# Later layernorms and transposes, token splits one per product, weight sums behind residual sums: an adaLN transformer block on one core

## The chip, the core and the metric

The kernel runs on one core of a Trainium2 chip. The metric is the device time of one execution in microseconds; several executions are timed and the median is taken. Beside them one execution is recorded by the hardware profiler; all views of the profile below are of that one.

The engines go by their short names: PE is TensorE (matmuls and transposes), DVE is VectorE, ACT is ScalarE, POOL is GpSimd, and SP is the engine whose queue issues nearly all transfers (DMAs). Each engine has a queue of its own and takes its instructions in that order. An instruction that waits holds up all that stands behind it on the same engine.

## What is computed

A transformer block with adaptive layernorm, for 2 batches of 1024 tokens of 1024 features, all in float32. Cut to what matters here:

```python
mod = (_silu(c) @ wmod).reshape(2, 6, 1, -1)
sa, ca, ga, sb, cb, gb = (mod[:, i] for i in range(6))      # ga, gb: kept at least 0.25 in size
h = _layernorm(x) * (1 + ca) + sa
x = x + ga * attention(h)
h = _layernorm(x) * (1 + cb) + sb
x = x + gb * ffn(h)

def attention(h):                       # 32 heads of 32, ALiBi bias, causal
    q, k, v = split(clip(h @ Wqkv.T, -8, 8))
    q, k = layer_norm(q) * q_ln_w + q_ln_b, layer_norm(k) * k_ln_w + k_ln_b
    return softmax(q @ k.T * scale + slopes * rel, causal) @ v @ Wout.T

def ffn(h):                             # 2752 inner features; Wg, Wu, Wd hold -1, 0, 1
    return ((silu(h @ Wg.T * ag) * (h @ Wu.T * au)) @ Wd.T) * ad
```

## The kernel before

**Products in seven.** Each large matrix product is done by a Strassen-Winograd scheme: the operands are cut in 2 by 2 blocks, sums and differences of the blocks are formed on DVE and POOL, and seven block products take the place of eight. `SEVEN` lists them in the order in which they are issued: P1, P2, U2, P5, U3, P53, U6, each with its bank of PSUM (`x` or `y`), its left operand (A11, A12, S2, S1, S3, S4, A22) and its right one (B11, B21, T2, T1, T3, B22, T4). Products of one bank build on each other, so after P1, U2 and P5 a copy on ACT (L972, L1305, L1751) saves the bank before the next product of that bank may start. The other four complete a quarter of the output each, read by DVE (L979, L977, L1313, L1311, L1756).

**Stages.** Modulation vectors; the q, k, v projections of batch 0; then attention of both batches, and beside it on the same engines the "dense" work: the projections of batch 1 and the output product with residual, layernorm and transposes of batch 0 and the first half of batch 1. `together` deals the two out to each other by estimated times. After attention comes the second half of the output product of batch 1 alone, then gate and up for batch 0 and batch 1 (11 "pairs" of 256 inner features each, the last of 192), then the down product.

**Order.** The scheduler of the framework orders the instructions of each engine by the order in which the program emits them and by when it reckons that their inputs are there. Where `pinned[0]` is set, PE keeps the emitted order; that is so from the start of attention on, except in pair 0 of batch 0. `behind(a, b)` adds an edge for that scheduler: `a` comes after `b` on its engine. It puts no wait into the program.

**Layernorm and transposes.** `normalize` takes the statistics of a block of 2 x 128 tokens on DVE (L706, L707) and returns `rest_`: on ACT a logarithm (L713) and an exponential (L717), on DVE five steps on two elements per partition (L711, L719 to L722) and two applies (L724). `Todo` holds what follows: `first` keeps `rest_` back as `due` or runs it at once, `place` runs it, and `run` issues one of the four groups of transposes (four 128 x 128 transposes by `turned`, L743, evacuated by DVE L860 and, in part, by ACT L862). `seven` calls `between` after half a product and after a whole one. `between` places the `due` layernorm at once, and issues transposes from product number `q0` on: 1 for batch 1 and the output product, 3 for the half of the output product after attention. Beside attention there is one PSUM bank for transposes.

**Output product.** `output` handles a block `j` of 256 tokens (four per batch, b and j in the names). `operand` loads the attention output of the next block at product 2 and, at product 6, scales it by the reciprocal sums (L1248) and forms its sums on DVE and POOL (L1249 to L1253). `read` multiplies by the gate and adds to the residual on POOL (L1314, L1315). The sum is stored, normalized, and transposed; `token_operands` forms the token side of gate and up from it (T1, T2 on DVE, T3, T4 on POOL, L1199 to L1202) and stores all seven operands on SP's queue (L1205).

**Attention.** `scores` issues the score products, exponentials (L1080) and, on diagonal blocks, a causal mask on POOL (L1084; the last one is kept in `last_mask`). `weigh` multiplies by v and adds the probabilities up on DVE and POOL (L1112).

**Gate and up.** Before each pair `weight_operands` turns the loaded weights into seven operands: three casts on ACT (L1635, L1636, L1643) and four sums on POOL (L1637, L1640 to L1642). For the very first pair the sum S1 goes behind `last_sum`, the last sum of the operand formed last. `tokens_in` loads one token operand (1 MB) on SP, casts it on ACT (L1549, the high part) and subtracts on DVE (L1550, the low part); both parts are multiplied. Batch 0's seven come from `token_tiles` while the output product of the last block runs, as its buffers come free. Batch 1's seven are emitted at the start of `gate_up(1)`, into the same buffers. Of the products of a pair, P2, P53, U3 and U6 give the four activation blocks; they and their sums (L1715) are stored on SP. `last_read` and `last_copy` remember the last bank read on DVE and the last bank copy on ACT, and `hold` puts an instruction behind `last_read`; only the checks of the weights use them.

The lines that set the places:

```python
def between(q):
    side(order.index(q))
    self.place()
    if order.index(q) >= q0:
        yield from self.run(n)
```

## Time and profile before

| | us |
|---|---|
| median of 3 runs | 2305.59 |
| their range | 2300.73 to 2306.57 |
| the profiled execution's own time | 2305.24 |
| its span, first to last instruction | 2303.5 |
| PE busy | 2159.4 (94%) |
| DVE busy | 1340.7 (58%) |
| POOL busy | 1106.8 (48%) |
| ACT busy | 944.7 (41%) |
| mean granted TensorE clock | 0.978 |

In the profile, stages can be told by the names of tiles: `bank<-wB,a` and `bank<-wT,a` are projections, `sc` and `av` scores and values, `bank<-wT_o,ao..` the output product, `gx`, `gy`, `ux`, `uy` gate and up, `dx`, `dy` the down product. Attention runs from about 360 to 1346 us, the output product of batch 1's last two blocks from 1351 to 1435, gate and up from 1416 to 2017, the down product from there to the end. A line of the timeline gives start, duration, engine, source line, operation, tiles, how many instructions were merged, and in brackets the idle time of the engine before it and what ended that.

### The profile page before, as it was taken

To read this page: it belongs to the slowest core of one execution; us is meant where nothing else is said; L and a number is where in the kernel's file an instruction comes from. 1 tells how busy PE (TensorE), PEld (TensorE's weight loads), DVE (VectorE), ACT (ScalarE), POOL (GpSimd) and SP (SyncE) were. 2 spreads that over 40 slices of the span, in tenths; PEclk is the share of its full clock that TensorE was granted. 3 is DMA by queue.
4 is the path that set the end of the run, shared out by engine and by line. 5 is a ranking of instruction groups with operands and counts; after the bars stand their busy time and mean duration, and the time that the engine had idled before them with its cause. 6 is when DMAs were issued, how large, how long until landed. Compare 5 with 4: busy or idle time off the path is not lost.

```text
span 2303.5 us, 27279 instructions
## 1 busy us (share of the span) xinstructions
PE 2159.4 (94%) x9537; PEld 1180.6 (51%) x9537; DVE 1340.7 (58%) x1843; ACT 944.7 (41%) x1782; POOL 1106.8 (48%) x775
## 2 busy tenths in 40 slices
PE   6999999999998899998888878899998999999998
PEld 2444443333333333332222234688876888788887
DVE  5775652455645543456557566887877654544544
ACT  1322224445344445555545522655554444323331
POOL 2330202443343464675575646488967767422212
PEclk9999999999999999999999989999999999999999
DMA  9887776536235531864443265778766786598765
GB/s 370 315 290 274 286 286 233 182 132 238 88 110 178 166 119 48 281 172 135 117 129 110 75 165 176 253 220 267 226 219 208 252 272 214 179 388 314 271 233 185
DMA packets 319350, 482.45 MB, mean 209 GB/s; under 512 B 16092, under 2 KB 235036, under 8 KB 310244
## 3 DMA queue, kind: packets, MB, share of 16 engines
q1 hardware_dynamic: 316752, 472.19, 60.8%
q10 hardware_dynamic: 2452, 8.43, 1.0%
q8 instruction: 77, 1.26, 0.2%
q14 instruction: 69, 0.57, 0.1%
HBM read 323.01 MB, written 157.55 MB: 209 GB/s over the span
## 4 chain that ended last, share of the span: by engine, by line
PE 40%; POOL 6%; issue 3%; DVE 3%; ACT 2%; DMA 1%; SPq 0%; POOLq 0%; ACTq 0%; DVEq 0%
PE dx L740 7%; PE gx L740 6%; PE ux L740 6%; PE dy L740 5%; PE uy L740 5%; PE gy L740 5%; PE bank L740 3%; PE sc L740 2%; ACT p L1080 2%; POOL p L1112 1%; DVE p L1112 1%; POOL xr L1315 1%; PE av L740 1%; DMA wst<-in_L_ffn_Wu_dram 1%; POOL aS L1715 1%
## 5 line engine op out<-in xcount | busy, mean ns | idle before, releaser
L1080 ACT ACTIVATE p<-sc,kw 128x128 f32<-128x128 f32 (+3 forms) x1024 | 422.5, 515 | 423.0 <-PE sc L740 409.5
L740 PE MATMUL bank<-wT,a 128*128 128x512 f32 x768 | 365.7, 609 | 14.4 <-ACT P L972 7.6
L1112 POOL TENSOR_TENSOR p<-p,p 128x1024 f32<-128x1024 f32 (+3 forms) x128 | 263.6, 2059 | 220.1 <-PE av L740 194.5
L1112 DVE TENSOR_TENSOR p<-p,p 128x1024 f32<-128x1024 f32 (+3 forms) x192 | 242.3, 1275 | 121.4 <-POOL p L1084 65.1
L740 PE MATMUL bank<-wB,a 128*128 128x512 f32 x576 | 275.4, 615 | 1.0 <-DVE raw L977 0.6
L740 PEld LDWEIGHTS bank<-wT,a 128*128 128x128 f32 x768 | 136.5, 191 | 193.9 <-issue 160.7
L1084 POOL TENSOR_SCALAR_AFFINE_SELECT p<-p 128x256 f32<-128x256 f32 x256 | 136.0, 544 | 199.2 <-ACT p L1080 193.1
L740 PE MATMUL sc<-cq,ck 32*128 32x512 f32 (+3 forms) x1536 | 189.3, 536 | 27.4 <-ACT p L1080 27.3
L740 PE MATMUL av<-p,cv 128*32 128x512 f32 (+3 forms) x1536 | 169.6, 505 | 12.1 <-POOL p L1084 12.0
L740 PEld LDWEIGHTS bank<-wB,a 128*128 128x128 f32 x576 | 103.8, 192 | 147.7 <-issue 132.3
L1840 DVE TENSOR_TENSOR lo<-lo,hi 128x1408 fp32r<-128x1408 f32 x56 | 95.0, 1699 | 92.2 <-ACT hi L1839 92.1
L740 PEld LDWEIGHTS sc<-cq,ck 32*128 32x128 f32 x1536 | 64.3, 184 | 164.4 <-issue 92.4
L1839 ACT CAST hi<-lo 128x1408 fp32r<-128x1408 f32 x56 | 76.9, 1375 | 136.9 <-DMA lo<-act 96.7
L1904 POOL TENSOR_TENSOR early_P<-early_P,x1in 128x512 f32<-128x512 f32 x16 | 37.2, 2323 | 164.1 <-DVE early_P L1902 159.4
L1637 POOL TENSOR_TENSOR wS<-wst,wst 128x1024 fp32r<-128x1024 f32 (+1 forms) x22 | 66.9, 3041 | 93.1 <-PE uy L740 72.7
L979 DVE TENSOR_TENSOR raw<-P,bank 128x512 f32<-128x512 f32 x48 | 32.9, 685 | 127.2 <-PE bank L740 117.0
L740 PEld LDWEIGHTS av<-p,cv 128*32 128x32 f32 x1536 | 32.6, 109 | 137.8 <-issue 81.5
L740 PE MATMUL gy<-hs,wS 128*128 128x512 f32 (+1 forms) x352 | 89.5, 396 | 7.9 <-ACT gP L1751 2.7
L740 PE MATMUL ux<-hs,wA 128*128 128x512 f32 (+1 forms) x352 | 88.7, 394 | 3.9 <-DVE uP L1756 3.9
L740 PE MATMUL gx<-hs,wA 128*128 128x512 f32 (+1 forms) x352 | 89.4, 394 | 1.5 <-DVE hs L1550 1.2
L740 PE MATMUL uy<-hs,wS 128*128 128x512 f32 (+1 forms) x352 | 89.3, 397 | 1.2 <-DVE uP L1756 1.2
L740 PE MATMUL gx<-hs,wS 128*128 128x512 f32 (+1 forms) x352 | 87.7, 390 | 2.3 <-ACT gU L1751 1.4
(269 smaller groups left out, 3994.9 us busy)
## 6 DMA issues: line engine op xcount, KB each, us to landing
lo<-act SPq DMA_DIRECT2D x56, 704.0 KB
a<-hop SPq DMA_DIRECT2D x20, 1792.0 KB
wm<-in_L_wmod_dram SPq DMA_DIRECT2D x48, 512.0 KB
act<-aS SPq DMA_DIRECT2D x88, 256.0 KB
wB<-in_L_attn_Wqkv_dram SPq DMA_DIRECT2D x21, 1024.0 KB
wst<-in_L_ffn_Wg_dram SPq DMA_DIRECT2D x40, 512.0 KB
wst<-in_L_ffn_Wu_dram SPq DMA_DIRECT2D x40, 512.0 KB
qk<-qs SPq DMA_DIRECT2D x16, 1024.0 KB
```

The lines of the kernel that those rows point to most:

```text
L740: return in_order(nc.tensor.matmul(*args, **kw_))
L979: nc.vector.tensor_add(dst, part_t[MATE[q]], bank)
L1080: last_exp[0] = nc.scalar.activation(p[:, g, lo:hi], sp[:, g, lo:hi], AF.Exp, bias=kw[:, d, h_ : h_ + 1])
L1084: last_mask[0] = nc.gpsimd.affine_select(out=p[:, :, 0:P], in_=p[:, :, 0:P], pattern=[[0, 2], [1, P]], compare_op=ALU.is_ge, fill=0.0, bas ...
L1112: adders[b](half, jb).tensor_add(dst, dst, ps[half][:, :, 0:n])
L1315: nc.gpsimd.tensor_add(xs[m][:, ts(n, HALF)], xs[m][:, ts(n, HALF)], yg)
L1637: ins = nc.gpsimd.tensor_add(f["S1"], raw["A21"], raw["A22"])
L1715: getattr(eng, op)(act[q], act[x_], act[y_])
L1839: nc.scalar.copy(hi, lo.bitcast(FP))
L1840: nc.vector.tensor_sub(lo, lo.bitcast(FP), hi.bitcast(FP))
L1904: eng.tensor_add(y, y, x1_of.pop(s))
```

## The change

- `normalize`: the small steps are folded. The first one also multiplies by -0.5, and after the exponential three steps follow (two multiplies and a fused add and multiply) where four stood.
- `between` no longer places the layernorm during product 0. `q0` becomes 2 for all projections (but the first of all) and the default of `output`, so transposes there start one product later. `normalize` in `output` runs at once only for batch 1's last block, not for its blocks 1 and 2 too.
- `masked` puts POOL's token sums (T3, T4), operand multiplies and operand sums behind the last mask emitted, while attention runs.
- `tokens_in` only loads; `tokens_split` does the cast and the subtraction, behind the last bank copy and the last bank read. Batch 0: two splits at once, the other five one per product in pair 0, each two products ahead of its use. Batch 1: a load after each product of batch 0's last pair, five splits in that pair and two in the first pair of batch 1.
- `last_sum`, behind which the first weight sum goes, becomes the last residual sum of batch 1's block 2.

```diff
@@ -692,6 +692,12 @@
 
     last_exp = [None]
     last_mask = [None]
+    beside = [False]
+
+    def masked(ins):
+        if beside[0]:
+            behind(ins, last_mask[0])
+        return ins
 
     def normalize(tiles, outs, small, nm):
 
@@ -708,18 +714,16 @@
 
         def rest_():
             ve = small.tile([P, n], FP, tag="ve", name=f"ve_{nm}")
-            nc.vector.tensor_scalar_add(ve, mv[:, :, 1], EPS)
+            nc.vector.tensor_scalar(ve, mv[:, :, 1], EPS, -0.5, ALU.add, ALU.mult)
             lv = small.tile([P, n], FP, tag="lv", name=f"lv_{nm}")
             ln = nc.scalar.activation(lv, mv[:, :, 1], AF.Ln, bias=eps_t)
             if last_exp[0] is not None:
                 behind(ln, last_exp[0])
             rstd = small.tile([P, n], FP, tag="rstd", name=f"rstd_{nm}")
             nc.scalar.activation(rstd, lv, AF.Exp, scale=-0.5)
-            fix = small.tile([P, n], FP, tag="fix", name=f"fix_{nm}")
-            nc.vector.tensor_mul(fix, rstd, rstd)
-            nc.vector.tensor_mul(fix, fix, ve)
-            nc.vector.tensor_scalar(fix, fix, -0.5, 1.5, ALU.mult, ALU.add)
-            nc.vector.tensor_mul(rstd, rstd, fix)
+            nc.vector.tensor_mul(ve, ve, rstd)
+            nc.vector.tensor_mul(ve, ve, rstd)
+            nc.vector.scalar_tensor_tensor(rstd, ve, 1.5, rstd, ALU.add, ALU.mult)
             for m, (t, o) in enumerate(zip(tiles, outs)):
                 nc.vector.tensor_scalar(o, t, mv[:, m, 0:1], rstd[:, m : m + 1], ALU.subtract, ALU.mult)
 
@@ -904,7 +908,8 @@
 
             def between(q):
                 side(order.index(q))
-                self.place()
+                if order.index(q) > 0:
+                    self.place()
                 if order.index(q) >= q0:
                     yield from self.run(n)
 
@@ -964,7 +969,7 @@
                     rawp.tile([P, D], FP, tag="raw", name=f"raw_{b}_{part}_{j}_{m}") for m in range(2)
                 ]
                 part_t = {}
-                q0, n = (2 - b, places) if b or part or j else (5, 4)
+                q0, n = (2, places) if b or part or j else (5, 4)
 
                 def read(q, bank):
                     if q in ("P1", "U2", "P5"):
@@ -1198,8 +1203,8 @@
         t = {q: pool.tile([P, KC // 2, P], FP, tag=f"t{q}", name=f"t{q}_{b}_{j}") for q in ("T4", "T3", "T2", "T1")}
         nc.vector.tensor_sub(t["T1"], b12, b11)
         nc.vector.tensor_sub(t["T2"], b22, t["T1"])
-        nc.gpsimd.tensor_sub(t["T3"], b22, b12)
-        nc.gpsimd.tensor_sub(t["T4"], b21, t["T2"])
+        masked(nc.gpsimd.tensor_sub(t["T3"], b22, b12))
+        masked(nc.gpsimd.tensor_sub(t["T4"], b21, t["T2"]))
         t.update(B11=b11, B21=b21, B22=b22)
         for i, q in enumerate(TOKEN_OPS):
             nc.sync.dma_start(hop2_dram[b][:, i, :, j], t[q])
@@ -1217,6 +1222,13 @@
             nc.sync.dma_start(wt_dram[3][:, r, i], w[:, at])
 
     last_sum = [None]
+    last_read = [None]
+    last_copy = [None]
+
+    def hold(ins, last=last_read):
+        if last[0] is not None:
+            behind(ins, last[0])
+        return ins
 
     def operand(b, j, ap_):
 
@@ -1245,12 +1257,14 @@
             nc.sync.dma_start(a[q], ao_dram[b][qb][:, ds(kh * 4, 4), ds(y0 + m * P, P)])
         yield
         for m, kh, q, eng in blocks:
-            eng.tensor_mul(a[q], a[q], rb[:, ds(kh * 4, 4), ts(m, P)])
+            ins = eng.tensor_mul(a[q], a[q], rb[:, ds(kh * 4, 4), ts(m, P)])
+            if eng is nc.gpsimd:
+                masked(ins)
         nc.vector.tensor_add(a["S1"], a["A21"], a["A22"])
         nc.vector.tensor_sub(a["S2"], a["S1"], a["A11"])
         a["S3"] = a["A21"]
-        nc.gpsimd.tensor_sub(a["S3"], a["A11"], a["A21"])
-        last_sum[0] = nc.gpsimd.tensor_sub(a["S4"], a["A12"], a["S2"])
+        masked(nc.gpsimd.tensor_sub(a["S3"], a["A11"], a["A21"]))
+        masked(nc.gpsimd.tensor_sub(a["S4"], a["A12"], a["S2"]))
         made[b, j] = a
         yield
 
@@ -1264,7 +1278,7 @@
 
     later = []
 
-    def output(b, js, pools, banks, bt, todo, keep, q0=1, after=None):
+    def output(b, js, pools, banks, bt, todo, keep, q0=2, after=None):
 
         gap_, ap_, tkp, partp, hbp, sm = pools
         while (b, 2 * js[0] * P // QB) not in settled:
@@ -1312,7 +1326,9 @@
                 else:
                     nc.vector.tensor_add(yg, yg, bank)
                     nc.gpsimd.tensor_mul(yg, yg, ga[:, ts(n, HALF)])
-                nc.gpsimd.tensor_add(xs[m][:, ts(n, HALF)], xs[m][:, ts(n, HALF)], yg)
+                ins = nc.gpsimd.tensor_add(xs[m][:, ts(n, HALF)], xs[m][:, ts(n, HALF)], yg)
+                if (b, j) == (B - 1, NJ - 2):
+                    last_sum[0] = ins
 
             yield from seven(lambda q, i: a[q][:, i, :], bt, banks, read, todo.places(q0, 1, ahead), 2)
             yield from todo.run(len(todo.list), True)
@@ -1321,7 +1337,7 @@
             for m in range(2):
                 nc.sync.dma_start(x1_dram[b * NT + qts[m]], xs[m])
             xn = xs
-            todo.first(normalize(xs, xn, sm, f"f{b}_{j}"), b == 1 and j >= NJ // 2 - 1)
+            todo.first(normalize(xs, xn, sm, f"f{b}_{j}"), b == 1 and j == NJ - 1)
             h2 = keep(b, j)
             for m in range(2):
                 for g in range(2):
@@ -1504,7 +1520,9 @@
             return LEAD + DENSE0 * a / att_us[0]
         return LEAD + DENSE0 + DENSE1 * (a - att_us[0]) / att_us[1]
 
+    beside[0] = True
     together(attention(apools, (halves, mostly), banks), dense_work(), share)
+    beside[0] = False
     att.close()
     opools, _, bt, todo, _ = out_args
     in_range()
@@ -1546,8 +1564,12 @@
         t = hs_tiles[b, i]
         raw = t[:, 1].bitcast(FP)
         token_load[0] = eng.dma_start(raw, hop2_dram[b][:, i].rearrange("p k j t -> p k (j t)"))
-        nc.scalar.copy(t[:, 0], raw)
-        nc.vector.tensor_sub(t[:, 1], raw, t[:, 0].bitcast(FP))
+
+    def tokens_split(b, i):
+        t = hs_tiles[b, i]
+        raw = t[:, 1].bitcast(FP)
+        hold(nc.scalar.copy(t[:, 0], raw), last_copy)
+        hold(nc.vector.tensor_sub(t[:, 1], raw, t[:, 0].bitcast(FP)))
 
     def own(stack, nm, bufs=1):
         return stack.enter_context(tc.tile_pool(name=nm, bufs=bufs, side="right", reuse_waits="tile"))
@@ -1561,6 +1583,8 @@
                 )
         for i in sorted(which):
             tokens_in(0, i)
+        for i in range(2):
+            tokens_split(0, i)
 
     def first_tokens():
         ost.close()
@@ -1576,14 +1600,6 @@
     low.close()
     late_pools.close()
 
-    last_read = [None]
-    last_copy = [None]
-
-    def hold(ins):
-        if last_read[0] is not None:
-            behind(ins, last_read[0])
-        return ins
-
     def small_integers(w, at, pool):
 
 
@@ -1593,9 +1609,7 @@
         j = small[0:n, 0 : int(np.prod(shape))]
         if len(shape) > 1:
             j = j.rearrange("p (a b) -> p a b", a=shape[0])
-        cast = nc.scalar.copy(j, w)
-        if last_copy[0] is not None:
-            behind(cast, last_copy[0])
+        hold(nc.scalar.copy(j, w), last_copy)
         hold(nc.vector.scalar_tensor_tensor(
             j, j, 0.0, w, ALU.add, ALU.not_equal, accum_out=count_a[0:n, at : at + 1]
         ))
@@ -1683,9 +1697,6 @@
 
             def gate_up(b):
                 tiles = [hs_tiles[b, i] for i in range(7)]
-                if b:
-                    for i in range(7):
-                        tokens_in(b, i)
                 for p in range(NPR):
                     n = PAIRS[p][1]
                     if p == 1:
@@ -1717,6 +1728,9 @@
                             keep_act(q, act[q])
 
                     for e, (c_, qa, qb_, q) in enumerate(SEVEN):
+                        split = {(0, 0): (0, e + 2), (0, NPR - 1): (1, e - 2), (1, 0): (1, e + 5)}.get((b, p))
+                        if split is not None and 0 <= split[1] < 7:
+                            tokens_split(*split)
                         if e == 3 and wdst is not None:
                             down_parts(p_, wdst)
                         if e == 4 and nb < B:
@@ -1755,6 +1769,8 @@
                                 t = part[mat, MATE[q]]
                                 last_read[0] = nc.vector.tensor_add(t[0:n], t[0:n], ps[0:n])
                                 done[mat] = t
+                        if (b, p) == (0, NPR - 1):
+                            tokens_in(1, e)
                         if q in QUAD:
                             m, h = QUAD[q]
                             ib = 2 * p + m
```

## The prediction

> **What bounds the kernel now.** I read five views in this order: the summary, the waits by engine, the timeline at each large wait, the windows around them, and the chain of waits.
>
> ```profile
> PE 40%; POOL 6%; issue 3%; DVE 3%; ACT 2%; DMA 1%; SPq 0%; POOLq 0%; ACTq 0%; DVEq 0%
> ```
>
> The chain that ended last is mostly PE: matmuls are issued in a fixed order and PE is busy 2159.4 of 2303.5 us, so time is gained where PE waits, 144 us in all. The waits of PE (total us, times, longest):
>
> ```profile
> PE sc L740 <- ACT p L1080: 27.3, 34, 2.8
> PE bank L743 <- DVE raw L724: 15.9, 3, 6.9
> PE av L740 <- POOL p L1084: 12.0, 5, 3.6
> PE bank L743 <- DVE h2t L860: 9.7, 4, 2.9
> PE bank L740 <- ACT oP L1305: 6.6, 1, 6.6
> PE bank L743 <- DVE xr L724: 6.6, 2, 4.3
> ```
>
> Five of these six rows are touched: L724 is the end of a layernorm (transposes wait for it), L1084 the causal mask, L1305 the copy that frees a bank of the output product. One of the long waits in the timeline:
>
> ```profile
> 703.51 9.06 POOL L1112 TENSOR_TENSOR p<-p,p 128x1024 f32<-128x1024 f32 x3 [15.99 <-PE av L740]
> 704.52 2.31 DVE L721 TENSOR_SCALAR fix_qk<-fix_qk 128x2 f32<-128x2 f32 x1
> 707.88 2.29 DVE L722 TENSOR_TENSOR rstd_qk<-rstd_qk,fix_qk 128x2 f32<-128x2 f32 x1
> ...
> 713.18 1.11 PE L743 MATMUL bank<-ident,raw 128*128 128x128 f32 x4 [6.89 <-DVE raw L724]
> 714.09 3.62 PE L740 MATMUL bank<-wB,a 128*128 128x512 f32 x4
> ```
>
> The two-element steps L721 and L722 take 2.3 us beside POOL's three adds; at 537 us, without them, they take 0.17. And the stall costs more than itself: four matmuls take 3.62 us after it against 1.98 before (the windows give a granted clock of 1.00 before it, 0.66 in it and 0.50 for the 5 us behind it). With the transposes (1.11 against 0.66) and the next scores and values (1.47 against 1.07) that is 2.5 us more per long stall.
>
> The end of the output product, after attention:
>
> ```profile
> 1399.37 2.34 POOL L1637 TENSOR_TENSOR wS<-wst,wst 128x1024 fp32r<-128x1024 f32 x1
> 1401.79 2.34 POOL L1640 TENSOR_TENSOR wS<-wS,wst 128x1024 fp32r<-128x1024 f32 x1
> 1404.09 1.26 POOL L1315 TENSOR_TENSOR xr<-xr,oP 128x512 f32<-128x512 f32 x1
> ...
> 1406.41 0.30 ACT L713 ACTIVATE lv_f<-mv_f,eps_t 128x2 f32<-128x2 f32 x1 [23.38 <-DVE mv_f L707]
> 1406.85 0.57 ACT L1305 COPY oP<-bank 128x512 f32<-128x512 f32 x1
> 1407.47 7.36 PE L740 MATMUL bank<-wT_o,aoS 128*128 128x512 f32 x12 [6.60 <-ACT oP L1305]
> ```
>
> Read upwards: PE waits for a copy, the copy stands on ACT behind a logarithm, that waits for statistics, these for a residual sum, and that stands on POOL behind two weight sums nobody needs yet. Last, the passage from batch 0 to 1 in gate/up, in the chain of waits:
>
> ```profile
> 1713.79 4.00 POOL wS L1637
> ...
> 1726.56 5.67 POOL wS L1642
> 1732.85 10.61 POOL aS L1715 x2
> ...
> 1745.61 6.97 DMA wst<-in_L_ffn_Wu_dram
> ```
>
> A steady pair of gate/up takes 25.4 us; by the starts of their first matmuls the three here take 28.16, 33.45 and 27.38. The last pair of a batch has 96-wide matmuls that run slower by themselves (2.00 against 1.98 per eight): 25.8. Lost: 2.4 + 8.0 + 2.0 = 12.4 us.
>
> **The change, part by part.**
>
> *T1, layernorm and transposes of batch 1's q and k.* The rest of the layernorm (one scale step, logarithm and exponential on ACT, the small DVE steps, two applies of 0.8 us) and the four groups of transposes with 16 evacuations of 0.4 us and the store are emitted one product later. The gap between the two stays one product, some 8 us with the attention work between. So a wait goes only where the new place meets no POOL adds. Today: 2.16 + 6.89 + 6.90 us and two slow spells of 2.5, 20.9 in all. I moved each of the eight by one product in the timeline: the logarithms now at 612 and 702 land near 620 and 709, inside the adds of 615.25 to 625.10 and 703.51 to 712.58; the one at 758 lands behind its adds, at 764; the other five meet none or one short add. Two of eight at some 5.5 us (a 4 us wait, half of it again as slow spell) leave 11: gain 10. Ends: 20.9 gained; or lost as in the rival below. The layernorm also has one DVE step fewer, 32 times 0.16 us, hidden as DVE is busy 58%; in the adds it counts 2.3, which is in the 5.5. The new fused last step has no row; nearest are L722's 0.16 and 2.29, and I take them.
>
> The Trainium skill speaks against this: "SBUF — State Buffer", section "Who interferes with whom", says that a DVE instruction with two SBUF inputs and a GpSimd one that reads SBUF exclude each other for the whole instruction. By it the three steps left after the exponential can each wait out an add of 3.0 us and the apply a fourth, an estimate of 12 us per layernorm that meets them, which would turn T1 into a gain of -3 and the total into 2286. The row of 2.3 decides for me.
>
> *T2, the same beside the output product.* Waits 4.30 and 2.28, and 1.17 of slow matmuls behind the first (3.15 against 1.98). Here the logarithm at 1070.96 had also held ACT 4.48 us for statistics behind the residual sums; a product later these are long there. The first goes (5.5), the second, whose chain took 8.5 us for other reasons (1222.55 to 1231.07), I leave. Gain 5.5, ends 7.7 and -7.7 (two new ones). The token sums and seven stores per block move with them, past the next operand's 8 loads on SP; those have a product and more until use. T2's evacuation waits (9.7) stay.
>
> *T3, masks first on POOL.* Up to 8 POOL operations per block are put behind the last mask. Of the five waits (12.0 us) four have such an operation directly ahead of the mask: 1.26 us at 1157 (wait 0.85), 1.26 at 1197 (3.07), 1.25 + 1.26 at 1271 (2.54), 1.79 at 1340 (3.60). The smaller of each pair: 0.85 + 1.26 + 2.51 + 1.79 = 6.4. The residual multiplies and adds (L1314, L1315) aren't moved and keep the rest. What is behind the moved ones: the operand sums for the next output block; PE waited for them once, 1.20 us. Ends: 12.0 gained, 6 x 1.2 = 7.2 lost.
>
> *T4, end of the output product.* Block 1's and 2's layernorm leave ACT's way, weight sums (3 x 2.34) go behind the residual sum. Waits of 2.60 (at 1373) and 6.60 go, and their slow spells: 5.40 against 3.70, and 7.36 for twelve against 5.3 (three quarters of 7.03 for sixteen): 13.0. Two I keep back for POOL's next residual multiply, now behind the weight sums. Gain 11; ends 13 and 0 (rival 2). The sums are needed by the third gate/up product, at 1426: hidden.
>
> *T5, first pair of gate/up.* From the end of the last output product (1434.6) to pair 1 (1470.15) PE needs 20.6 us of gate/up (25.4 less what ran before) and 2.6 of transposes: 12.3 lost. The 5 later splits (cast 1.91, subtraction 2.29) now come two products (7.3 us) ahead and behind bank reads; 2.12 lost to a read (uP L1756) goes. Waits for the loads themselves and three table loads of 1.28 stay. Gain 2; ends 12.3 and -8.4 (two splits exposed).
>
> *T6, batch passage.* Seven loads of 1 MB and 14 split steps, none added. DVE reads behind splits cost PE 1.77 + 1.71 + 1.17 = 4.65; these go. But where the stall goes: PE then comes 3.1 us earlier to the copy at 1750.65, which ACT holds behind a cast waiting for the weight load of 1745.61, and that follows POOL's chain above, which no edit shortens. Gain 1.5. Ends: 12.4, and -3.4 (the seventh load behind the activation stores on SP until 1741.1, then 5.0 landing, 1.91, 2.27: 1750.3 against its use at 1746.9).
>
> **Sum.** 10 + 5.5 + 6.4 + 11 + 2 + 1.5 = 36.4. In the stretch beside the output product PE also waits for scores' exponentials (the 27.3 row); a third of T2 and T3, 4.0, I let come back there. Net 32.4. The profiled execution took 2305.24 (span 2303.5 and 1.7 around it), 0.35 under the median, so both bases agree: 2273.
>
> **Rivals.** A measurement of this kernel tells 0.3% (7 us) from nothing.
> 1. *Waits only move* beside attention: scores and evacuations take T1 to T3's place. For it: the 27.3 and 9.7 rows; against it: the long stalls have a clock penalty that nothing replaces. Gain 14.5: 2291.
> 2. *A hidden transfer:* pair 0 waits for token loads (SP waited 14.7 us for output products to free their space), so T4 and T5 give nothing. Against it: the loads follow those products, which come earlier. Gain 10 + 5.5 + 6.4 - 4.0 + 1.5 = 19.4: 2286.
> 3. *Slower: layernorms land in POOL's adds.* Place: the fourteen beside attention; price 6.9 + 2.5 = 9.4 each. Against today's 28.6 (20.9 + 7.7) and the other gains of 20.9 it decides from 9.4n - 28.6 - 20.9 > 7, seven of fourteen: 2305.2 + 65.8 - 49.5 = 2321.5. The adds cover about 10 of 48 us per group, so seven is far.
> 4. *It doesn't do what it says:* the edits give the scheduler an order, and it may issue nearly what it did (batch 1's loads already come at 1706, before their place in the code): 2305.
>
> **Numbers.** Forecast 0.50, rivals 0.17, 0.12, 0.11, 0.10. Faster: 0.48 + 0.15 + 0.11 + 0.01 = 0.75; slower 0.11 + 0.02 = 0.13; same 0.12. Time: 2273. Its own range is 2262 (T1 at its good end) to 2284 (T4 at its bad one). The whole range runs from 2253 (T1, T3, T4, T5 and T6 half way to their good ends: 5.5 + 2.8 + 1 + 5.1 + 5.4 = 19.8) to 2306, above which lie rival 3 and part of rival 4.
>
> **What will show it.** The raw L724 row falls below 12 us and xr L724 below 3; oP L1305 below 1; L1084 to about 6; weight sums start after the residual sum of block 2; the three pairs at the batch passage lose some 11 us still, with the ACT cast waiting for the weight load. Wrong if the layernorm's small steps take 2.3 us in most places, if the first pair starts no earlier, or if PE's wait for exponentials grows by more than 10 us.

## The result and the profile after

The changed kernel takes 2295.8 us in the median (2292.95 to 2308.14), the kernel before, timed with it, 2304.85 (2300.35 to 2307.17): a ratio of 0.9972 over all runs, 95% interval 0.9959 to 0.9985. That is 9 us less by the medians and 6 by the ratio, where 32 were forecast. The profiled execution took 2292.95, its span is 2291.1 (2303.5 before). In the changed kernel the lines have moved: L724 (apply) is now L728, L722 (the last small step) is L726, L707 (end of the statistics) is L713, L713 (logarithm) is L719, L740 and L743 (matmuls and transposes) are L744 and L747, L1311/1313 (reads of the output's banks) are L1325/1327, L1084 is L1089, L1305 is L1319, L860 is L864, L1080 is L1085, L1112 is L1117, L1315 is L1329, L1637/1640 are L1651/1654.

The waits of PE in the changed kernel (total us, times, longest):

```profile
PE sc L744 <- ACT p L1085: 25.8, 32, 2.2
PE bank L747 <- DVE raw L728: 18.0, 4, 5.9
PE av L744 <- POOL p L1089: 11.9, 6, 4.0
...
PE spare_ps L744 <- ACT oP L1319: 4.4, 1, 4.4
PE bank L747 <- DVE xr L728: 4.3, 2, 2.7
PE bank L747 <- DVE h2t L864: 3.8, 5, 1.6
PE bank L744 <- DVE oP L1327: 3.5, 2, 1.9
...
PE bank L744 <- ACT oP L1319: 2.5, 1, 2.5
```

Of the five rows that the change touches, the evacuations' (h2t, 9.7 to 3.8) and the normalized residual's (xr, 6.6 to 4.3) fell. The raw row grew, from three waits to four. The mask row stayed. The copies' two waits at the end of the output product, 2.60 and 6.60 before, are now 4.4 and 2.5, but 3.5 us for the reads (L1327) stand beside them, where 0.4 stood before.

Where the time went is told best by landmarks that both traces have: the copies of finished attention blocks, the output product's copies, and in gate/up the activation that reads bank gx, which belongs to the last product of a pair. The table gives how far the profiled execution of after is ahead of that of before, and what each stretch added.

| landmark (after) | ahead, us | added in the stretch | forecast for it |
|---|---|---|---|
| 799.7, end of batch 1's q and k blocks | -4.9 | -4.9 | T1: +10 |
| 1047.8, v blocks and two output blocks later | -3.4 | +1.5 | with the next |
| 1331.1, end of attention, four output blocks later | +14.7 | +18.1 | T2 + T3 - 4.0: +7.9 |
| 1406.9, last copy of the output product | +10.2 | -4.5 | T4: +11 |
| 1452.5, last product of gate/up's first pair | +13.4 | +3.2 | T5: +2 |
| 1798.6, three pairs past the batch passage | +13.0 | -0.4 | T6: +1.5 |
| 2291.1, end | +12.4 | -0.6 | 0 |

So the net hides parts of both signs: one part lost, one gained more than twice its forecast, and the 11 us forecast for the end of the output product aren't there.

**The part that lost.** One of the four raw waits in the timeline of the changed kernel:

```profile
665.66 0.31 ACT L719 ACTIVATE lv_qk<-mv_qk,eps_t 128x2 f32<-128x2 f32 x1
...
667.41 8.04 POOL L1117 TENSOR_TENSOR p<-p,p 128x1024 f32<-128x1024 f32 x3 [15.94 <-PE av L744]
667.45 3.38 DVE L1117 TENSOR_TENSOR p<-p,p 128x1024 f32<-128x1024 f32 x1
...
670.75 2.29 DVE L726 SCALAR_TENSOR_TENSOR rstd_qk<-ve_qk,rstd_qk 128x2 f32<-128x2 f32 x1
...
673.58 3.15 DVE L728 TENSOR_SCALAR raw<-raw,mv_qk,rstd_qk 128x1024 f32<-128x1024 f32 x2
...
676.06 1.11 PE L747 MATMUL bank<-ident,raw 128*128 128x128 f32 x4 [5.87 <-DVE raw L728]
...
676.96 3.62 PE L744 MATMUL bank<-wT,a 128*128 128x512 f32 x4
```

It is the picture of before at another place: a two-element step of 2.29 us beside POOL's adds, an apply that ends 11 us after the logarithm, PE waiting, and slow matmuls (3.62) behind it. One of attention's adds on DVE itself (3.38) also stands ahead of that step. After the change four layernorms meet the adds, with logarithms at 619.83, 665.66, 720.72 and 772.06, where three waits stood before. The long step of each ends with an add on POOL: at 624.02, 673.05, 725.52 and 776.91, where adds end at 624.00, 673.03, 725.50 and 776.89. So its length, 1.70 to 2.29 us, is what is left of the add that it meets.

**The part that gained**, by the windows of each stretch (us of the window, its length, busy us and instructions of PE, PEld, DVE, ACT and POOL, granted clock, transfers). Before:

```profile
1044.00:1346.00 302.00, 255.14 (x1352) 81.74 (x1356) 182.56 (x242) 152.92 (x351) 184.11 (x146) 0.94 0.38 110
```

After:

```profile
1048.00:1331.00 283.00, 246.49 (x1344) 78.34 (x1344) 186.15 (x232) 151.55 (x348) 186.89 (x146) 0.95 0.41 121
```

PE's idle time falls from 46.9 to 36.5 us; its waits ahead of transposes alone, summed inside these windows, from 16.3 to 6.8. Its busy time falls by 8.7. Some 3.8 of that are eight matmuls (four transposes of 0.30 and four row sums of 0.65) that stand behind the end of attention after the change: they moved into the next stretch, whose loss of 4.5 is mostly they. But 4.5 are the same 60 matmuls of one operand at 658 ns instead of 734: the slow spells behind the waits went with them. Waits for masked probabilities are the same, 12.0 and 11.9.

**The end of the output product**, after:

```profile
1390.33 1.26 POOL L1329 TENSOR_TENSOR xr<-xr,oP 128x512 f32<-128x512 f32 x1 [1.60 <-DVE oP L1325]
1391.55 2.34 POOL L1651 TENSOR_TENSOR wS<-wst,wst 128x1024 fp32r<-128x1024 f32 x1
...
1392.66 0.29 ACT L719 ACTIVATE lv_f<-mv_f,eps_t 128x2 f32<-128x2 f32 x1 [19.72 <-DVE mv_f L713]
...
1393.10 0.57 ACT L1319 COPY oP<-bank 128x512 f32<-128x512 f32 x1
...
1393.71 5.40 PE L744 MATMUL bank<-wT_o,aoS 128*128 128x512 f32 x8 [2.48 <-ACT oP L1319]
```

The weight sum did go behind the residual sum. But the logarithm still stands ahead of the copy on ACT, though the program now emits it later, and waits 19.72 us there for its statistics; the same at 1360.88, where PE then waits 4.42.

**The passage between the batches**, after:

```profile
1727.13 0.92 SPq L1720 DMA_DIRECT2D act<-aS  x2
...
1732.29 1.05 SPq L1550 DMA_DIRECT2D wst<-in_L_ffn_Wu_dram  x1
...
1736.51 1.04 ACT L1649 CAST wA<-wst 128x1024 fp32r<-128x1024 f32 x1 [8.23 <-DMA wst<-in_L_ffn_Wu_dram]
1737.46 0.58 ACT L1765 COPY gP<-gy 128x512 f32<-128x512 f32 x1
...
1738.18 2.54 PE L744 MATMUL gy<-hs,wS 128*128 128x512 f32 x8 [2.52 <-ACT gP L1765]
```

As before the change, the weight load comes behind activation stores on SP, the cast waits for it, and the bank copy stands behind the cast.

### The profile page after: what moved, and what is told of

It is laid out like the page before. It is cut to its first block, busy times and chain, and to the rows that moved or that the text cites. A ratio compares the mean times of both kernels' runs of the same rounds, so it can differ in the third digit from the quotient of the medians.

```text
span 2291.1 us, 27269 instructions
## 1 busy us (share of the span) xinstructions
PE 2153.7 (94%) x9537; PEld 1176.6 (51%) x9537; DVE 1353.3 (59%) x1811; ACT 943.8 (41%) x1782; POOL 1105.1 (48%) x775
## 5 line engine op out<-in xcount | busy, mean ns | idle before, releaser
L1085 ACT ACTIVATE p<-sc,kw 128x128 f32<-128x128 f32 (+3 forms) x1024 | 421.5, 514 | 394.2 <-PE sc L744 381.9
L744 PE MATMUL bank<-wT,a 128*128 128x512 f32 x768 | 371.7, 618 | 14.0 <-ACT P L977 7.7
L1117 POOL TENSOR_TENSOR p<-p,p 128x1024 f32<-128x1024 f32 (+3 forms) x128 | 262.4, 2050 | 242.0 <-PE av L744 214.8
L1117 DVE TENSOR_TENSOR p<-p,p 128x1024 f32<-128x1024 f32 (+3 forms) x192 | 240.3, 1266 | 107.9 <-POOL p L1089 49.4
L744 PE MATMUL bank<-wB,a 128*128 128x512 f32 x576 | 270.6, 606 | 1.5 <-DVE raw L984 0.9
L744 PEld LDWEIGHTS bank<-wT,a 128*128 128x128 f32 x768 | 138.7, 194 | 196.2 <-issue 164.1
L1089 POOL TENSOR_SCALAR_AFFINE_SELECT p<-p 128x256 f32<-128x256 f32 x256 | 134.3, 536 | 214.6 <-ACT p L1085 201.2
L744 PE MATMUL sc<-cq,ck 32*128 32x512 f32 (+3 forms) x1536 | 187.3, 540 | 25.9 <-ACT p L1085 25.8
L744 PE MATMUL av<-p,cv 128*32 128x512 f32 (+3 forms) x1536 | 169.7, 507 | 12.0 <-POOL p L1089 11.9
L744 PEld LDWEIGHTS bank<-wB,a 128*128 128x128 f32 x576 | 102.3, 189 | 149.8 <-issue 136.6
L744 PEld LDWEIGHTS sc<-cq,ck 32*128 32x128 f32 x1536 | 63.3, 185 | 160.7 <-issue 91.2
L1651 POOL TENSOR_TENSOR wS<-wst,wst 128x1024 fp32r<-128x1024 f32 (+1 forms) x22 | 66.0, 3001 | 90.5 <-PE uy L744 69.1
L744 PEld LDWEIGHTS av<-p,cv 128*32 128x32 f32 x1536 | 32.5, 109 | 137.4 <-issue 79.2
L744 PE MATMUL gy<-hs,wS 128*128 128x512 f32 (+1 forms) x352 | 88.9, 394 | 7.4 <-ACT gP L1765 2.5
L744 PE MATMUL gx<-hs,wS 128*128 128x512 f32 (+1 forms) x352 | 88.1, 391 | 4.1 <-ACT gU L1765 1.9
L744 PE MATMUL gx<-hs,wA 128*128 128x512 f32 (+1 forms) x352 | 89.1, 394 | 1.9 <-ACT h2t L866 1.5
L744 PE MATMUL ux<-hs,wA 128*128 128x512 f32 (+1 forms) x352 | 87.7, 390 | 2.3 <-DVE uP L1770 2.3
L744 PE MATMUL uy<-hs,wS 128*128 128x512 f32 (+1 forms) x352 | 88.4, 394 | 1.1 <-DVE uP L1770 1.1
```

What stands on the lines that cost most here:

```text
L744: return in_order(nc.tensor.matmul(*args, **kw_))
L1085: last_exp[0] = nc.scalar.activation(p[:, g, lo:hi], sp[:, g, lo:hi], AF.Exp, bias=kw[:, d, h_ : h_ + 1])
L1089: last_mask[0] = nc.gpsimd.affine_select(out=p[:, :, 0:P], in_=p[:, :, 0:P], pattern=[[0, 2], [1, P]], compare_op=ALU.is_ge, fill=0.0, bas ...
L1117: adders[b](half, jb).tensor_add(dst, dst, ps[half][:, :, 0:n])
L1651: ins = nc.gpsimd.tensor_add(f["S1"], raw["A21"], raw["A22"])
```

## The experiments

Every ratio is to the kernel before, timed in the same batch of runs. "Undone" means: as in the kernel before.

### Which part gained, which lost

**e1: T1 undone.** Only the projections go back to product 0 and `q0 = 2 - b`; `at` is 0 for them and 1 for the output product.

```diff
-                if order.index(q) > 0:
+                if order.index(q) >= at:
-                q0, n = (2, places) if b or part or j else (5, 4)
+                q0, n = (2 - b, places) if b or part or j else (5, 4)
```

> The changed kernel, with the layernorm of batch 1's q and k placed during product 0 and their transposes from product 1 on, as before; all else as changed. My theory: the move of the projections lost time (four waits of 18.0 us in place of three of 15.9; the attention outputs came 4.9 us later from 795 us on), so undoing it gives 3 to 6 us more: ratio to before 0.9935 to 0.995, PE waits for raw back at 14 to 16 us in three. Rival: the later place is neutral and the lag was made up in the next stage anyway: ratio 0.997 as the changed kernel.

Measured: 2285.58 us, 0.9911 (0.9895 to 0.9928). The raw row is 13.3 in three waits. T1 cost the changed kernel 6 us by the profiled executions and 14 by the ratios. From the attention copy that stands at 536 us in the changed kernel to the end of the q and k blocks it takes 255.5 us, the changed kernel 263.5, the six other runs with the same projections (e3, e4, e6, e7, e8, e10) 264 to 267, the kernel before 259.2. That e1 is 4 us under the kernel before there fits the folded steps: its wait near 713 us is 4.5 us instead of 6.9, with one small step of 2.3 us there instead of two.

**e2: the kernel before with T2 alone.** Its layernorm at product 1 and `q0 = 2` in the output product, nothing else.

> The kernel before, with one edit: in the output product the layernorm is placed from product 1 and the transposes from product 2 on (beside attention; the half after attention keeps its 3 for transposes). My theory: this one edit holds the whole gain, because between 1044 and 1346 us the changed kernel makes up 18 us and nowhere else any: 14 to 20 us faster than before, ratio 0.991 to 0.994, and no lag in the projections. Rival: the gain needs the masks moved ahead on POOL too: 0 to 6 us, ratio 0.9975 to 1.0.

Measured: 2291.79 us, 0.9942 (0.9921 to 0.9963). At the end of attention it is 19.1 us ahead of before, 16.5 of them gained in the stretch of the four output blocks. This edit by itself holds the whole gain of the change. Up to the last output copy it loses 6 us again: the eight matmuls that moved there (3.8), and copies' waits of 7.7 and 4.5 us. At the last product of gate/up's first pair it is 16.1 us ahead.

**e3: T3 undone.** `masked` returns its argument.

> The changed kernel without the order that puts POOL's operand and token sums behind the last mask. My theory: PE's wait for masks was 12.0 us before and 11.9 after, so that edit did nothing: ratio 0.996 to 0.998. Rival: it is behind part of the 18 us gained beside the output product, and without it the kernel loses 6 to 10 us: ratio 1.000 to 1.002.

Measured: 2300.52 us, 0.9984 (0.9970 to 0.9997), against 0.9972 with it: 3 us, inside the overlap of the intervals. PE's waits for masks are 10.2 us without it and 11.9 with it. The order that I priced at 6.4 us of those waits doesn't shorten them; a few us elsewhere are not excluded.

**e6: the splits of T5 and T6 undone.**

```diff
-    def tokens_split(b, i):
-        t = hs_tiles[b, i]
-        raw = t[:, 1].bitcast(FP)
-        hold(nc.scalar.copy(t[:, 0], raw), last_copy)
-        hold(nc.vector.tensor_sub(t[:, 1], raw, t[:, 0].bitcast(FP)))
+        nc.scalar.copy(t[:, 0], raw)
+        nc.vector.tensor_sub(t[:, 1], raw, t[:, 0].bitcast(FP))
```

> The changed kernel with the splitting of the token operands of gate and up as before the change (each split with its load, all seven of a batch together). My prediction gave this part 2 us in batch 0's first pair and 1.5 us at the passage to batch 1. Theory from the traces (the first pair's silu stands 13.4 us ahead of the kernel before, just as far as the last output copy did, and the three pairs at the passage take 27.9, 30.6 and 28.1 us against 27.6, 30.8 and 28.3): nothing, within 1.5 us of the changed kernel's 2296. Rival (the split is worth its 3.5 us and more, hidden by something else that got longer): 2299 us or more.

Measured: 2299.95 us, 0.9983 (0.9971 to 0.9996): 1.1 thousandths, 2.5 us, above the changed kernel, inside the overlap. From the last output copy to the last product of gate/up's first pair it takes 48.1 us. That distance is 48.2 before the change and 45.0 after it, but also 45.1 in e2, which has no such split, and 47.9 in e1, which has it. So the 3 us don't come from the split; from what they come isn't shown. The passage takes as long as with it.

**e10: the weight sums' place undone**, behind the last operand sum again.

> The changed kernel, with the first weight sums of gate and up on GpSimd tied behind the last operand sum, as before the change, instead of behind the residual sum of block 2. Theory 1 (the order of GpSimd's work at the end of the output product was worth nothing, because there the logarithm still stands ahead of the copies on ScalarE, and gate and up starts at the same distance from the last copy before and after the change): within 2 us of the changed kernel, 2294 to 2298 us. Theory 2 (my prediction's: the weight sums ahead of the residual sum hold the layernorm of the last two blocks): 2300 us or more, and the last output copies come 4 us or more later than in the changed kernel, measured from the end of attention.

Measured: 2301.64 us, 0.9998 (0.9985 to 1.0011). That is 6 us above the changed kernel; the intervals just touch. The copies' waits are 7.7 + 4.5, as in e2, against 2.5 + 4.4, but the reads' are 0.9 against 3.5. From the end of attention to the last output copy it takes 77.5 us (e2: 77.4), the changed kernel 75.8, eight other runs with the new place and no other edit there 74.1 to 76.1. So this half of T4 is worth some 2 us by the traces, less than half of the 4 us that the second theory asked for. The rest of the 6 isn't the edit's by the trace: 7 us of lag were there at the end of attention, before the weight sums come.

### Why the projections lost: place or distance

**e5: three products between layernorm and transposes**, at 0 and 3 (`at` as in e1).

```diff
-                if order.index(q) > 0:
+                if order.index(q) >= at:
-                q0, n = (2, places) if b or part or j else (5, 4)
+                q0, n = (2 + b, places) if b or part or j else (5, 4)
```

> The changed kernel, but the layernorms of batch 1's queries and keys go back to the start of the next block, as before the change, and their transposes start a product later than in the changed kernel (product 3 instead of 2; before the change, product 1). So three products lie between the layernorm and its first transpose, two before the change, one or two after it. Theory (TensorE loses time in these blocks because the transposes come while the layernorm still waits for its turn on VectorE, so distance is what counts): TensorE's waits for the raw tile, 18.0 us after the change, 15.9 before and 13.3 with this part of the change undone, fall below 4 us, and the kernel takes 10 to 18 us less than the changed one, 2278 to 2286 us, 1 to 8 us less than with the part undone. Rival (the waits only move: the transposes now crowd the last products, and the query tile that is stored, or the next block's layernorm, comes late instead): 2286 us or more, raw waits gone but others of like size beside them.

Measured: 2274.52 us, 0.9879 (0.9860 to 0.9899), 21 us less than the changed kernel. No wait for the normalized raw tile (L728) is left. Waits for the evacuations of these transposes (qs) grew from 2.6 to 6.5 us: of the rival's waits that only move, some came.

**e9: three products as well, at 1 and 4.**

```diff
-                q0, n = (2, places) if b or part or j else (5, 4)
+                q0, n = (2 + 2 * b, places) if b or part or j else (5, 4)
```

> The changed kernel, with batch 1's layernorms of queries and keys where the change put them (at product 1), but their transposes from product 4 instead of 2: the same three products between the two as in the run that placed them at products 0 and 3, only both a product later. Theory 1 (the distance between layernorm and first transpose is what counts; where the layernorm's own steps land costs nothing, because nothing waits for them): within 3 us of that run, 2272 to 2281 us, TensorE's waits for the raw tile below 3 us. Theory 2 (the place counts as well: from product 1 on the layernorm falls into GpSimd's three sums of the raw tile, its small steps take 2.3 us instead of 0.15, and the transposes have only products 4 to 6 left): 2282 to 2294 us, with waits of 5 us and more for the raw tile, or for the query tile that is stored from the transposes.

Measured: 2274.24 us, 0.9872 (0.9849 to 0.9895), the same as e5, with no raw wait either. Its timeline shows a layernorm that meets the adds just as in the changed kernel:

```profile
660.28 0.31 ACT L719 ACTIVATE lv_qk<-mv_qk,eps_t 128x2 f32<-128x2 f32 x1
...
662.03 8.07 POOL L1117 TENSOR_TENSOR p<-p,p 128x1024 f32<-128x1024 f32 x3 [16.58 <-PE av L744]
...
665.38 2.32 DVE L726 SCALAR_TENSOR_TENSOR rstd_qk<-ve_qk,rstd_qk 128x2 f32<-128x2 f32 x1
...
668.23 3.15 DVE L728 TENSOR_SCALAR raw<-raw,mv_qk,rstd_qk 128x1024 f32<-128x1024 f32 x2
...
677.32 0.66 PE L747 MATMUL bank<-ident,raw 128*128 128x128 f32 x4
```

The step still takes 2.32 us and the apply still ends 11 us after the logarithm. Only the transposes come 17.0 us after the logarithm; in the changed kernel they were due 4.5 us after it (676.06 less the wait of 5.87, less 665.66). So nobody waits. With one product between the two the place told (e1 against the changed kernel); with three, no wait for the tile is left at either place. How far behind the layernorm the first transpose stands decides. A distance of two wasn't tried here. The windows of the stretch give both prices. After:

```profile
536.00:800.00 264.00, 243.72 (x1097) 87.50 (x1094) 148.70 (x243) 110.17 (x270) 99.14 (x75) 0.96 0.46 156
```

and e9:

```profile
540.00:777.00 237.00, 235.36 (x1090) 83.74 (x1089) 149.94 (x236) 109.13 (x269) 101.69 (x75) 1.00 0.50 169
```

The stretch is 27 us shorter. PE's waits for DVE there fall from 20.3 to 1.6 us; its busy time falls by 8.4 for nearly the same matmuls, at a granted clock of 1.00 instead of 0.96.

In the traces the place isn't quite without account at this distance either: in the stretch from that attention copy to the end of the q and k blocks (see e1), the three runs with 0 and 3 (e5, e11, e12) take 245 to 247 us, the four with 1 and 4 (e9, e13, e14, e15) 237 to 239. The waits for evacuations there are 6.0 to 6.8 against 1.6 to 2.3 us. The ratios of e5 and e9 don't show it, those of e11 and e13 do.

### Whether the end of the output product can give anything

**e4: the logarithm tied behind the last copy.**

```diff
+            if out_copy[0] is not None:
+                behind(ln, out_copy[0])
```

> The changed kernel, with the layernorm's logarithm also ordered behind the last bank copy of the output product on ACT. My theory: the scheduler still put the logarithm ahead of the copy that PE waits for, so the waits of 4.42 and 2.48 us and their slow matmuls (6.45 and 5.40 against 3.70) stayed: they go, 8 to 12 us faster than the changed kernel, ratio 0.992 to 0.9938. Rival: the first pair of gate and up waits for its token loads anyhow, so the time before it is worth nothing: ratio 0.997.

Measured: 2297.68 us, 0.9965 (0.9951 to 0.9980), no different from the changed kernel. The copies' waits are gone, and this stands in their place:

```profile
1369.65 0.69 DVE L713 BATCH_NORM_STATS2 st_f<-xr 128x6 f32<-128x512 f32 x1 [1.38 <-POOL xr L1332]
...
1371.77 1.60 DVE L731 TENSOR_SCALAR xr<-xr,mv_f,rstd_f 128x1024 f32<-128x1024 f32 x2
...
1373.29 0.68 DVE L1330 TENSOR_TENSOR oP<-oP,bank 128x512 f32<-128x512 f32 x1
...
1374.03 3.78 PE L747 MATMUL bank<-wT_o,aoS 128*128 128x512 f32 x4 [3.41 <-DVE oP L1330]
```

The read of the bank stands on DVE behind the statistics and the applies of the same layernorm, which wait for the same residual sum. Two engines stood in the way, and the first hid the second. The row for these reads grew from 3.5 to 9.7 us.

**e7: the layernorm two products later, tied behind copies and reads**, in the last two blocks (product 3, transposes from 4). The logarithm is tied behind the last copy, the first DVE step behind the last read.

> The changed kernel, but in the last two blocks of batch 1's output product the layernorm of the block before is issued two products later (at product 3), its transposes from product 4, two per place, and its logarithm and its first VectorE step are tied behind the last copy and the last VectorE read of the product's banks. Theory (the wait of TensorE for the output's copies and reads, 6.9 + 1.9 us after the change, 17 us with the logarithm alone tied behind the copies, is there because the layernorm waits for the residual sum on GpSimd and stands ahead of the copies on ScalarE and ahead of the reads on VectorE; so both have to be moved): both waits fall below 2 us in sum, the kernel takes 5 to 10 us less than the changed one, 2286 to 2291 us. Rival (the end of the output product is set by the chain residual sum, layernorm, transposes, token sums, stores, loads of gate and up, and a later layernorm only lengthens it): the two waits are gone, but the start of gate and up comes no earlier, 2294 to 2302 us, with a longer wait for the token operands or for mv.

Measured: 2300.55 us, 0.9985 (0.9970 to 0.9999): no gain. The copies' and reads' waits fell to 1.7 us, and PE waited 5.4 for evacuations of the transposes. In the trace the way from the end of attention to the last product of gate/up's first pair is 2.7 us shorter than after the change.

**e12: the same at product 2, transposes from 3**, on top of e11 below.

> The two gaining edits together, and in the last two output blocks the layernorm placed at product 2 and its transposes from product 3, with the logarithm and the first VectorE step tied behind the product's copies and reads. Placed at product 3 with transposes from 4 this removed the copies' and reads' waits but gave 5.4 us back where the evacuation of the transposes stood on VectorE behind the next block's operand products, which waited for their load. Theory (a product earlier, the evacuations go ahead of that load's waiters): waits of TensorE from the last scores to the last output copy below 5 us, 4 to 8 us less than without it, 2263 to 2269 us. Rival (the chain residual sum, layernorm, transposes, stores, loads sets the end there, whatever stands where): 2269 us or more.

Measured: 2270.55 us, 0.9853 (0.9829 to 0.9877), against 0.9869 for e11: the intervals overlap. What stands in the way now:

```profile
1349.31 5.62 SPq L1263 DMA_DIRECT2D aoA<-ao  x4
...
1357.86 0.69 DVE L1266 TENSOR_TENSOR aoA<-aoA,rb 128x512 f32<-128x512 f32 x1 [3.18 <-DMA aoA<-ao]
1358.47 1.36 DVE L870 TENSOR_SCALAR h2t<-bank,modt 128x128 f32<-128x128 f32 x4
...
1359.98 0.63 PE L753 MATMUL bank<-ident,xr 128*128 128x128 f32 x4 [2.80 <-DVE h2t L870]
```

The evacuation stands on DVE behind the next block's operand product, and that waits for its load. Beside it PE waits 5.1 us for the normalized residual there. From the end of attention to the last product of gate/up's first pair the gain is 3 us.

**e15: those loads a product earlier** (on top of e14 below).

> The run before, and in the last two output blocks the layernorm at product 2 with its logarithm and first VectorE step tied behind the product's copies and reads, and the loads of the next block's operand issued a product earlier (at product 1 instead of 2), since without that TensorE's evacuations stood behind products that waited 3.2 us and more for these loads. Theory: TensorE's waits from the end of attention to the last output copy, 9 to 13 us in every run so far, fall below 5 us, and the kernel takes 4 to 8 us less than the run before it. Rival (a chain from the residual sum through layernorm, transposes, token sums, stores and loads sets the start of gate and up): the waits move to gate and up's first pair (hs, uP), and the time is within 2 us of the run before it.

Measured: 2273.06 us, 0.9856 (0.9834 to 0.9878), against 0.9862 for e14. That row is gone, and the wait that is left is for the normalized residual (5.9 us). In each of four attempts (e4, e7, e12, e15) the wait was removed where I named it and another stood in the same stretch: for a read behind the layernorm, for evacuations behind an operand's load, for the normalized residual itself. The traces gain 1 to 3 us there each time, which the ratios don't tell from nothing. That a shorter chain from the residual sum to the transposes would gain wasn't tried.

### The passage, and what adds up

**e8: four stores of activation sums behind the weight load.** In batch 0's last pair the stores of S1 to S4 are kept in a list and issued after the load for batch 1's pair 1.

> The changed kernel, but the stores of four activation sums of batch 0's last pair of gate and up are issued on SyncE's queue behind the weight load for batch 1's pair 1 instead of ahead of it. Theory (the three pairs at the passage take some 10 us more than others because that load stands on SyncE behind stores that wait for GpSimd's sums, and GpSimd sums weights first; so the weights, their cast on ScalarE and the copies queued behind it come late): 4 to 10 us less than the changed kernel, 2286 to 2292 us, TensorE's waits at the passage, 10.1 us, fall below 5. Rival (the passage is set by the work there, the last sums and the splits on VectorE and ScalarE, not by the load): within 1.5 us of the changed kernel's 2296, the load earlier and the waits the same.

Measured: 2293.82 us, 0.9956 (0.9938 to 0.9973). In its timeline the load is ahead of the stores:

```profile
1733.03 0.50 SPq L1550 DMA_DIRECT2D wst<-in_L_ffn_Wu_dram  x1
...
1733.62 5.42 SPq L1724 DMA_DIRECT2D act<-aS  x4
...
1737.29 1.04 ACT L1649 CAST wA<-wst 128x1024 fp32r<-128x1024 f32 x1 [1.23 <-DMA wst<-in_L_ffn_Wu_dram]
```

Counted from the activation of that last pair's last product (1723.2 here, 1715.0 after the change), the cast starts at 14.1 instead of 21.5 us. PE's waits at the passage fall from 9.1 to 5.0 us, and the three pairs take 6 us less in the trace. The intervals of the ratios, 0.9956 and 0.9972, overlap; but the five later runs with this edit (e11 to e15) gain 5.5 to 6.2 us at the passage in their traces too.

**e11: e5 and e8 together.**

> The changed kernel with the two edits that gained by themselves: batch 1's layernorms of queries and keys at product 0 with transposes from product 3 (that alone 0.9879 of the time of before), and the four stores of activation sums behind the weight load at the passage (alone 0.9956, where the changed kernel stands at 0.9972). If they add up (they lie in stages 700 us apart): 0.986 to 0.987 of the time of before, 2268 to 2273 us. If the wait at the passage comes back in another form: 2274 us, as with the first alone.

Measured: 2271.29 us, 0.9869 (0.9848 to 0.9891). In the trace both gains are there, 17 us at the end of the q and k blocks and 6 us at the passage.

**e13: e9 and e8 together.**

> The changed kernel with batch 1's transposes of queries and keys from product 4 (layernorm at product 1, as the change has it; alone 0.9872 of the time of before) and the four activation sums' stores behind the weight load at the passage (worth 6 us there by the trace). Theory (the two lie 700 us apart and add up): 0.984 to 0.9865, 2265 to 2271 us. If the passage's wait comes back in another form: 0.987, 2273 us.

Measured: 2263.37 us, 0.9812 (0.9789 to 0.9835): 44 us under the kernel before, and the fastest of all. It is more than the two parts promised; its profiled execution (2270.76) is the slowest of its five, so the trace doesn't show from where the rest comes. Against e11 it is 8 us less, and 7 of them stand in the traces' stretch of the q and k blocks (239.2 against 246.5 us).

**e14: on top of e13, the output product's transposes from product 3.**

```diff
-            todo.places(q0, 1, ahead), 2)
+            todo.places(3, 1, ahead), 2)
```

> The run before, and the transposes of every output block from product 3 instead of 2 (its layernorm stays at product 1). Theory (distance counts here as in the projections): TensorE's waits for the normalized tile and for its evacuations beside attention, some 7 us, fall below 3 us, and with the lower clock behind each of them the kernel takes 4 to 10 us less than the run before it: 2257 to 2266 us. Rival (beside attention the stretch is set by the exponentials, the masks and the adds; these waits are hidden or come back as waits for p): within 2 us of the run before it, with waits for p that grow by as much as the others fall.

Measured: 2275.74 us, 0.9862 (0.9834 to 0.9890), 12 us slower than e13; the intervals just touch. Only one product more lies between layernorm and transposes here, two instead of one. PE's waits in e13:

```profile
PE sc L744 <- ACT p L1085: 25.4, 32, 2.2
PE av L744 <- POOL p L1089: 10.4, 6, 4.0
...
PE bank L747 <- DVE xr L728: 5.3, 2, 3.7
```

and in e14:

```profile
PE sc L744 <- ACT p L1085: 30.6, 29, 5.1
PE av L744 <- POOL p L1089: 12.6, 7, 4.0
...
PE bank L744 <- DVE oP L1327: 5.8, 2, 3.9
```

The wait for the normalized residual is gone, as asked. The waits for exponentials and masks grew by 7.4 us and the waits for the bank reads from 1.9 to 5.8. The stretch of the four output blocks takes 296.8 us (296.7 in e15, which has the same edit) against 286.1 in e13. So the rule of the projections doesn't carry over to this stage as it stands: the rival's mechanism held, waits that come back as waits for p, though not its time, which was within 2 us of e13.

## Why the prediction was wrong

The sign was right, and 2295.8 lies inside 2253 to 2306; the size was 9 of 32 us by the medians and 6 by the ratio. By its own steps:

**T1 is the step that failed: +10 forecast, -4.9 in the trace, -6 to -14 by e1.** The failing sentences are "I moved each of the eight by one product in the timeline" and "the other five meet none or one short add". The layernorm at 656.65, which I let go free, lands near 665 when it is moved by some 8 us, and the timeline of before already has three long adds there:

```profile
663.67 9.92 POOL L1112 TENSOR_TENSOR p<-p,p 128x1024 f32<-128x1024 f32 x3 [15.94 <-PE av L740]
```

It came to 665.66 and met the adds at 667.41. Nor do the adds keep their places: PE's value products release them (the bracket of that row), and PE's order with all that hangs on it moved too. The adds that were at 703.51 are at 715.58 after the change, those at 754.73 at 762.94, and the layernorm reckoned for 764, behind its adds, came at 772.06, inside them. So four layernorms met the adds, not the two that I priced (at 620 and 709), and the four waits alone came to 18.0 us against the 11 that I had left for waits and slow spells together. The deeper fault lies in the sentence before: I kept "the gap between the two stays one product" as harmless and asked only where the layernorm lands. e9 shows that a layernorm in the adds leaves no wait for its tile with a gap of three products, and e5 against e1 that the gap gains at the other place as well. The signs on record said so too: small steps of 1.7 to 2.3 us in four of the eight places.

The rule of the Trainium skill that I weighed there ("SBUF — State Buffer", "Who interferes with whom") gave an estimate of -3 for T1, nearer than mine, but by luck. It got there by three long steps and a long apply for each of two layernorms. The trace has one long step of 1.7 to 2.3 us for each of four, and at three of them one apply of 2.4 to 2.9 us instead of 0.8. The rule itself agrees with the trace: each long step ends 0.02 us behind an add of POOL. What the estimate had wrong is that every step would meet a whole add of its own.

**T2: the mechanism was right, the size too small.** 5.5 forecast; T2 and T3 together less 4.0 were 7.9, and the stretch gained 18.1, of which e2, with T2 alone, has 16.5. I took the wait of 4.30 with its spell and left the evacuations ("T2's evacuation waits (9.7) stay"): those fell to 3.8, and 4.5 us of slow matmuls went with all the waits. About 14 of the 18 are gained (9.5 of waits and 4.5 of slow matmuls); the rest is the 3.8 us of matmuls that moved into the next stretch, which the prediction didn't count.

**T3: 6.4 forecast, none in its row.** The masks' wait is 11.9 after, 12.0 before, 10.2 without the edit (e3). The moved operations did leave, but one that I had left in its place stands directly ahead of the mask now, at three of the four long waits a residual add (L1329):

```profile
1191.63 1.26 POOL L1329 TENSOR_TENSOR xr<-xr,oP 128x512 f32<-128x512 f32 x1
...
1192.84 0.77 POOL L1089 TENSOR_SCALAR_AFFINE_SELECT p<-p 128x256 f32<-128x256 f32 x2
```

The prediction said of the residual multiplies and adds that they "keep the rest"; they kept all of it.

**T4: 11 forecast, -4.5 in its stretch, of which 3.8 are the matmuls that T2 moved there.** "Block 1's and 2's layernorm leave ACT's way" took the place of emission for the place in the queue. The scheduler put the logarithm ahead of the copy again; that is rival 4, in one part. And the forecast would have failed without that: with the logarithm out of the way the bank read took its place (e4), then the evacuation (e7, e12), then the layernorm itself (e12, e15). The half about the weight sums was right in kind, but worth some 2 us in the traces (e10).

**T5 and T6: 3.5 forecast, nothing found** (e6, 2.5 us at the edge of what can be told). The 3.2 us gained in T5's stretch come and go without the splits. For T6 the prediction's own reason held: the passage is set by the weight load behind POOL's sums and the stores; e8 moved that load and gained.

The 4.0 let come back were not needed: waits for exponentials fell from 27.3 to 25.8. Rival 3, layernorms in the adds, was the right mechanism for T1 at four places instead of seven; rival 1's time (2291) is nearest, but what it says didn't happen beside attention.

## What to carry to other kernels

When a producer and its consumer are moved together, their distance is unchanged, and the wait between them need not go (here 15.9 us before, 18.0 after). Move the consumer away from the producer first (here +2 products against the change, 21 us), stage by stage, since the same kind of move beside the output product lost 12 us, and count on the neighbours moving along. Before pricing a wait at its length, find the second engine on which the same late value is also waited for: four edits at the end of the output product each removed the named wait and gained no more than 3 us in the traces. A later place in the program is not yet a later place in the engine's queue.

## What the hardware showed unexpectedly

A stretch of some 260 us with four waits of 3.6 to 5.9 us has a granted clock of 0.96, the same work without them 1.00, and PE's busy time for nearly the same matmuls is 243.7 against 235.4 us; I had counted 2.5 us for each long stall, and over four that is about what it is, but the short waits of T2's stretch carry such a cost as well (734 against 658 ns for 60 matmuls). And a two-element DVE step that starts beside one of POOL's adds lasts until that add ends, for the new fused step (2.29 us, to 673.05, the add to 673.03) as for the plain ones (1.70, to 624.02, the add to 624.00); the steps between the adds take 0.14 to 0.35.
